# Column sums of x from the transposed blocks, and where the fold of W_self stands: a two-layer graph network on one core

## The chip, the core and the metric

The kernel runs on one core of a Trainium2 chip. The time is device microseconds of that core for one execution: the median of 3 runs of the kernel before is 706.46 us (703.6 to 707.98). The core has these engines, each with its own queue, worked off in order: TensorE (PE in the profile; its weight loads are PEld), VectorE (DVE), ScalarE (ACT), GpSimd (POOL) and SyncE (SP, which here only issues DMAs). GpSimd and ScalarE issue DMAs too.

## The reference

4096 nodes, 512 features, and an adjacency matrix in which about one entry in 1024 is set (some four neighbours a node). Layer 0 is graph attention with 8 heads of 64; layer 1 takes the mean over neighbours. Each ends with a residual sum and a layer norm without weights.

```python
# layer 0
Wh = einsum('nf,hfo->hno', x, W)
f1, f2 = Wh . a[:, :64], Wh . a[:, 64:]
e = where(adj > 0, leaky_relu(f1[:, :, None] + f2[:, None, :], 0.2), -9e15)
out = einsum('hnm,hmo->hno', softmax(e), Wh)
x = layernorm(x + out)
# layer 1
agg = mask @ x / max(deg, 1)
combined = concat([x @ W_self + b_self, agg @ W_nb + b_nb])
x = layernorm(x + relu(combined @ W_comb + b_comb))
```

Two things of it matter here. A node without a neighbour gets, by the softmax over equal values, the mean of Wh over all nodes, and this needs the column sums of x. And layer 1 is linear up to the relu, so W_self times the upper half of W_comb (called W_c1 here) and W_nb times its lower half can be multiplied once, ahead of time; the kernel calls this a fold, and the two products m1 and m2.

## The kernel before

The nodes are worked on in 32 blocks of 128 rows (NB = 32, P = 128). x stays in SBUF as `xs`. The order of all instructions is written out by hand: each engine works off its own in the order in which the Python code emits them. There are three stages.

**Stage 1 (lines 839 to 986), the lists.** Loop b over 29 blocks, the last ones behind it. For each block of 128 adjacency rows, SyncE loads two tiles of 1 MB (`load_adj`, four buffers `at`, issued two blocks ahead), ScalarE turns them into bf16 masks (`mask_adj`, L412), PE folds the masks into keys in PSUM (`fold_adj`, L430) which ScalarE first fills with column numbers (`key_bank`, L422), and VectorE picks the largest keys (`max_keys`, L445). Four blocks together are then decoded into lists of neighbours (`decode`, a generator that is taken a step at a time through `some(lists)`, four steps in a block); it is mostly small VectorE instructions (L454 to L538), and it ends by narrowing four tiles of owners to one byte (`of`, L516 on GpSimd for the first six groups, L518 on ScalarE for the others). `late_lists` adds a few steps from b = 16 on.

In the same loop a node block w is computed: `transposed` puts x transposed into PSUM (`tp`, one buffer, L346) and copies it to SBUF on ScalarE (`xT`, L348); `node_half` multiplies it with w_sb, twice (L354), VectorE copies each half out (L358), `node_rest` takes small pieces (L361, L362 on VectorE, L365 on GpSimd), and `store` writes the row to the table t0 in DRAM through GpSimd's DMA queue (L928). In two blocks, those in AHEAD = (14, 19), two node blocks are computed, so that the nodes end two blocks ahead of the lists. `sum_x` (L340) adds each block of x into `xacc` on GpSimd, four blocks after its load was issued. `mean_row` (from b = 25) makes the row for nodes without neighbours from it.

The fold of W_self lies here as well. `load_fold(0, ...)` loads W_self and W_c1, 1 MB each, ahead of the second block of x (L851). `fold_halves` is a generator that is taken one step in most odd blocks: `turned` transposes a quarter of W_self (L270) and copies it on ScalarE (L271) into parts of `xs` that are not loaded yet, PE multiplies in halves (L283), ScalarE copies the first half (L288) and VectorE adds the second (L290). `fold_bias` adds b_self times W_c1 into `brow`, four VectorE instructions (L322).

**Stage 2 (to line 1064), layer 0.** At its turn W_nb and the lower half of W_comb are folded in the same way in quarters (`fold_quarters`, L270, L303, L307). Then for each block five gathers of rows of t0 (`gather`, L610, each a DMA issued by GpSimd; five buffers), the attention weights, the sums on VectorE and PE (L692 to L720), a layer norm on ScalarE (L727 to L736), a transpose (L346), the product with m2 (`a_z`, L741), and two stores through SyncE: the product's row to t1, the transposed block to xt. `sum_bias` (i = 7) spreads `brow` over the partitions.

**Stage 3 (to line 1141), layer 1.** The same five gathers a block, now from t1. The first five blocks' gathers are limited to early rows, so that they can be issued before stage 2 has ended; six late gathers add the rest. Seven buffers: the gathers of block b + 7 follow `g_shared(b)` and `g_adds(b)`. PE does `g_self` (x times m1, eight matmul records of L773 a block) two blocks ahead and `g_shared` (L780, four records); VectorE and ScalarE do the rest (L754 to L800, `g_norm`).

The code of the functions follows; names there: `ps` is the PSUM pool, in which a tile of a name with `bufs=1` has to be read before the next of that name is written.

Of the kernel before, what the change touches and what calls it, by code (L numbers as in the profile page):

```python
# [31 lines left out]
F32 = mybir.dt.float32  # L32
# [8 lines left out]
P = 128  # L41
# [49 lines left out]
def listed_layers(  # L91
# [32 lines left out]
    EX = KX + 2 + 1  # L124
    AHEAD = (14, 19)
    FIRST = (0, 1, 3)
    LB = NB - 2

# [120 lines left out]

    def load_fold(k, w, fp, eng):  # L250
        wr = fp.tile([P, FB, HD], F32, name="wr")
        eng.dma_start(wr, w.rearrange("(c p) o -> p c o", p=P))
        wc = fp.tile([P, FB, HD], F32, name="wc")
        eng.dma_start(
            wc, w_comb[k * HD : (k + 1) * HD, :].rearrange("(c p) o -> p c o", p=P)
        )
        return wr, wc
# [9 lines left out]
    def turned(wr, c, wT):  # L267
        tp = ps.tile([P, FB, P], F32, name="sm", bufs=2)
        for d in range(FB):
            nc.tensor.transpose(tp[:, d, :], wr[:, c, ts(d, P)], ident)  # L270
        nc.scalar.copy(wT, tp.rearrange("p c r -> p (c r)"))  # L271
        return wT.rearrange("p (c r) -> p c r", c=FB)

    def fold_halves(loaded, m, place):

        wr, wc = loaded
        wT = turned(wr, 0, place(0))
        yield
        for c in range(FB):
            for k in range(2):  # L280
                mp = ps.tile([P, HD], F32, name="nm", bufs=2)
                for d in range(2 * k, 2 * k + 2):
                    nc.tensor.matmul(  # L283
                        mp, lhsT=wT[:, d, :], rhs=wc[:, d, :], start=(d == 2 * k),
                        stop=(d == 2 * k + 1),
                    )
                if k == 0:
                    nc.scalar.copy(m[:, c, :], mp)  # L288
                else:
                    nc.vector.tensor_add(m[:, c, :], m[:, c, :], mp)  # L290
                    if c + 1 < FB:
                        wT = turned(wr, c + 1, place(c + 1))
                yield

    def fold_quarters(loaded, m, place):

        wr, wc = loaded
        wT = turned(wr, 0, place(0))
        for c in range(FB):
            nxt = turned(wr, c + 1, place(c + 1)) if c + 1 < FB else None  # L300
            mp = ps.tile([P, HD], F32, name="tp", bufs=1)
            for d in range(FB):
                nc.tensor.matmul(  # L303
                    mp, lhsT=wT[:, d, :], rhs=wc[:, d, :], start=(d == 0), stop=(d == FB - 1)
                )
                if d == FB - 1:
                    nc.scalar.copy(m[:, c, :], mp)  # L307
                yield
            wT = nxt
# [27 lines left out]

    def sum_x(b, xacc):
        if b < NB:
            nc.gpsimd.tensor_tensor(xacc, xacc, xs[:, b, :], OP.add)  # L340

    def transposed(b, wp, tag="tp"):

        tp = ps.tile([P, FB, P], F32, name=tag, bufs=1)
        for c in range(FB):
            nc.tensor.transpose(tp[:, c, :], xs[:, b, ts(c, P)], ident)  # L346
        t = wp.tile([P, FB, P], F32, name="xT", bufs=2)
        nc.scalar.copy(t, tp)  # L348
        return t
# [18 lines left out]

    def mean_row(w_sb, xacc, wp):

        pm = ps.tile([P, FB], F32, name="sm", bufs=2)
        for c in range(FB):
            nc.tensor.matmul(
                pm[:, c : c + 1], lhsT=xacc[:, ts(c, P)], rhs=inv_n, start=True, stop=True
            )
        xm = small.tile([P, FB], F32, name="xm", bufs=1)
        nc.vector.tensor_copy(xm, pm)
        yield
# [68 lines left out]
    def decode(b0, dp, place):  # L447
# [66 lines left out]
        for g in range(G):  # L514
            if b0 + 2 * G < LB:
                nc.gpsimd.tensor_copy(of[:, b0 + g, :], sts[g])  # L516
            else:
                nc.scalar.copy(of[:, b0 + g, :], sts[g])  # L518
        nc.vector.tensor_copy(es[:, bs], pe[:, :, :, 0:EX])
# [296 lines left out]

    wp = ctx.enter_context(tc.tile_pool(name="work", bufs=1))
    fp_cm = tc.tile_pool(name="fold", bufs=1, side="right")
    fp = fp_cm.__enter__()
    oo_cm = tc.tile_pool(name="owners", bufs=1, side="right")  # L820
    oo = oo_cm.__enter__()
# [28 lines left out]
    brw = load_bias()  # L850
    loaded = load_fold(0, w_self, fp, nc.sync)  # L851
    load_x(1)
# [7 lines left out]
    nc.scalar.dma_start(brow[0:1, :], b_comb.rearrange("(a o) -> a o", a=1))  # L860
    xacc = xa.tile([P, FIN], F32, name="xacc")
    nc.gpsimd.memset(xacc, 0.0)
    pa = []
# [3 lines left out]
    nc.scalar.copy(av[:, 0], pa[0])  # L867
    xT = transposed(0, wp)

# [22 lines left out]
    summed(1, 1, pr1[1])  # L892
    m1s = fold_halves(loaded, m1, lambda c: xs[:, (NB - 12, NB - 11, NB - 4, NB - 3)[c], :])
    next(m1s)
    key_bank(0)
    for h in range(NH):
        mask_adj(0, h)
    bcol = bias_columns(brw)
    biased = fold_bias(loaded, bcol[:, 0:FB])
    for b in range(XL // 2):  # L900
        sum_x(b, xacc)

# [15 lines left out]
    def on_last(b):  # L918
        if b % G == 0:
            last[0] = fp.tile([P, FB, HD], F32, name="wc").rearrange(  # L920
                "p c (k r) -> p (c k) r", k=2
            )
        return last[0][:, b % G, :]
# [7 lines left out]
    for b in range(LB - 1):  # L931
        for k in range(1 + (b in AHEAD)):
            load_x(w + k + XL)
            sum_x(w + k + XL // 2, xacc)
        load_adj(b + 2, ap)
# [4 lines left out]
        for k in range(1 + (b in AHEAD)):  # L940
            nxt = transposed(w + 1, wp)
            if k == 0:
                key_bank(b + 1)
                for h in range(NH):
                    mask_adj(b + 1, h)
            node_block(w, xT, None if k else b)
            w, xT = w + 1, nxt
        for k in range(2):
            some(lists)
        if b == 0 or b % 2:  # L950
            next(m1s, None)
        if 1 <= b <= 4:
            next(biased)
        if b == 16:
            lates = late_lists(dp, fp.tile([P, FB * HD // P, P], F32, name="wr"))
        if b >= 16:
            next(lates, None)
        if b == 25:
            pieces = mean_row(w_sb, xacc, wp)
        if b >= 25:  # L960
            next(pieces, None)
# [5 lines left out]
    mask_adj(LB, 0)  # L967
    loaded = load_fold(1, w_nb, fp, nc.sync)
    fold_adj(LB - 1, dp)
# [13 lines left out]
    for k in range(4):  # L983
# [8 lines left out]
    gps += [gather_buffer(k) for k in range(2, GA)]  # L992
    m2 = loaded[0]
    m2s = fold_quarters(
        loaded, m2, lambda c: wp.tile([P, FW], F32, name="row", bufs=2)[:, 0:FIN]
    )
    a_owners(0, wp)
# [15 lines left out]
    for i in range(-2, NB + 1):  # L1013
# [45 lines left out]
        if i in (-1, 0):  # L1059
            for k in range(2):  # L1060
                next(biased)
        if i == 7:
            sum_bias()

# [16 lines left out]
    for b in range(2):  # L1081
# [3 lines left out]
        g_adds(b, G1[b], wq)  # L1085
        G1[b + GB] = gather(t1, b + GB, gps[b])
    for b in range(2):
        nxt = load_xT(b + 1, wp)
# [25 lines left out]
    for b in range(NB):  # L1114
# [20 lines left out]
        if b == 4:  # L1135
# [4 lines left out]
            nc.vector.tensor_add(flag, fl[:, 0:1], fl[:, 1:2])  # L1140
    g_norm(NB - 1, wp)
@with_exitstack
def dense_layers(
# [390 lines left out]
```

## Time and profile before

| | us |
|---|---|
| median of 3 runs | 706.46 |
| the profiled execution | 702.09 |
| its span, first to last instruction | 699.8 |
| mean granted clock of TensorE | 0.962 |
| PE busy, share of the span | 624.7 (89%) |
| DVE busy | 521.4 (75%) |
| ACT busy | 440.5 (63%) |
| POOL busy | 397.8 (57%), of which gathers L610 277.5 + 28.5, sum_x L340 40.9 |
| DMA | 209.64 MB, mean 300 GB/s |

The profile is of one execution. Its lines give for a group of instructions: the line of the kernel, engine, operation, output and inputs by the program's names, the shapes, the count, then busy time and the mean duration of one in ns, then the idle time of the engine just before them and what ended most of it. In the timeline a line is: start in us, duration, the same names, and in brackets the idle time before it and what ended it. In a table of stretches the columns are: start:end, length, busy us and count of PE, PEld, DVE, ACT and POOL, granted clock of TensorE (1.00 is full), the DMA engines' busy share, and GB/s. The busy time of PE is modelled, as its matmuls overlap. "issue" is time in which an engine waited for nothing that the profile shows.

The 40 slices of the page (17.5 us each) show where the stages lie:

```profile
GB/s 269 408 407 408 409 407 408 406 362 276 258 363 337 333 225 211 223 236 215 258 263 277 285 275 277 283 275 215 276 281 301 296 311 309 310 312 314 311 280 108
```

The first eight slices are stage 1 with the DMA at one constant rate, the next six the rest of stage 1 at lower rates; stage 2 begins in slice 15 or so, stage 3 in slice 29.

### The profile page before, as it was taken

To read this page: it belongs to the slowest core of one execution; us is meant where nothing else is said; L and a number is where in the kernel's file an instruction comes from. 1 tells how busy PE (TensorE), PEld (TensorE's weight loads), DVE (VectorE), ACT (ScalarE), POOL (GpSimd) and SP (SyncE) were. 2 spreads that over 40 slices of the span, in tenths; PEclk is the share of its full clock that TensorE was granted. 3 is DMA by queue.
4 is the path that set the end of the run, shared out by engine and by line. 5 is a ranking of instruction groups with operands and counts; after the bars stand their busy time and mean duration, and the time that the engine had idled before them with its cause. 6 is when DMAs were issued, how large, how long until landed. Compare 5 with 4: busy or idle time off the path is not lost. (4 is left out here: it accounts for less than half of the span.)

```text
span 699.8 us, 9126 instructions
## 1 busy us (share of the span) xinstructions
PE 624.7 (89%) x2350; PEld 345.6 (49%) x2350; DVE 521.4 (75%) x1416; ACT 440.5 (63%) x922; POOL 397.8 (57%) x468
## 2 busy tenths in 40 slices
PE   4899998977889787888999999999989999999982
PEld 2566666755567453454555555555434444444330
DVE  6258999896998885889889989989555566666552
ACT  1668878663767722566767777667536667676653
POOL 6342434323232277756667776756677777777771
PEclk9899999999999969899999999999999999999996
DMA  8999999997799977777888889986889899989983
GB/s 269 408 407 408 409 407 408 406 362 276 258 363 337 333 225 211 223 236 215 258 263 277 285 275 277 283 275 215 276 281 301 296 311 309 310 312 314 311 280 108
DMA packets 91973, 209.64 MB, mean 300 GB/s; under 512 B 13694, under 2 KB 13702, under 8 KB 91914
## 3 DMA queue, kind: packets, MB, share of 16 engines
q1 hardware_dynamic: 63024, 114.05, 44.2%
q0 software_dynamic: 28704, 94.66, 43.2%
q8 instruction: 21, 0.34, 0.2%
q14 instruction: 38, 0.31, 0.1%
q10 hardware_dynamic: 186, 0.28, 0.1%
HBM read 175.25 MB, written 33.69 MB: 299 GB/s over the span
## 5 line engine op out<-in xcount | busy, mean ns | idle before, releaser
L610 POOL DMA_INDIRECT g<-t,idx x290 | 277.5, 957 | 114.2 <-issue 54.6
L354 PE MATMUL pw<-w_sb,xT 128*128 128x264 f32 x512 | 135.5, 411 | 16.9 <-DVE row L358 16.9
L412 ACT ACTIVATE ab<-at 128x2048 bf16<-128x2048 int32 x64 | 122.0, 1908 | 29.6 <-DMA at<-in_adj_dram 20.8
L354 PEld LDWEIGHTS pw<-w_sb,xT 128*128 128x128 f32 x512 | 97.3, 200 | 47.5 <-DVE row L358 20.0
L741 PE MATMUL pw<-wr,xT 128*128 128x512 f32 x256 | 117.8, 603 | 0.7 <-ACT xT L348 0.7
L365 POOL COPY f1s<-lst 128x24 f32<-128x24 f32 x32 | 8.4, 262 | 136.9 <-DVE lst L361 69.1
L692 DVE TENSOR_TENSOR g<-g,key 128x1024 f32<-128x1024 f32 x64 | 77.9, 1217 | 1.1
L741 PEld LDWEIGHTS pw<-wr,xT 128*128 128x128 f32 x256 | 46.4, 191 | 47.3 <-issue 46.4
L704 PE MATMUL nm<-g,own 128*128 128x512 f32 x128 | 65.8, 638 | 0.0
L348 ACT COPY xT<-tp 128x512 f32<-128x512 f32 x64 | 37.4, 585 | 34.8 <-PE tp L346 34.7
L773 PE MATMUL nm<-m,xT 128*128 128x512 f32 x128 | 57.6, 593 | 1.5 <-DMA xT<-xt 1.5
L773 PE MATMUL pw<-m,xT 128*128 128x512 f32 x128 | 57.6, 593 | 0.0
L727 ACT ACTIVATE xs<-y,ln_sum 128x512 f32<-128x512 f32 x32 | 23.1, 722 | 48.6 <-DVE y L720 48.6
L346 PE MATMUL tp<-ident,xs 128*128 128x128 f32 x256 | 41.3, 286 | 10.5 <-ACT xs L736 8.1
L346 PEld LDWEIGHTS tp<-ident,xs 128*128 128x128 f32 x256 | 31.1, 147 | 36.5 <-ACT xs L736 24.6
L340 POOL TENSOR_TENSOR xacc<-xacc,xs 128x512 f32<-128x512 f32 x32 | 40.9, 1279 | 11.1 <-DMA xs<-in_x_dram 10.5
L358 DVE COPY row<-pw 128x264 f32<-128x264 f32 x64 | 27.1, 424 | 26.5 <-PE pw L354 21.3
L796 DVE SCALAR_TENSOR_TENSOR sm<-y,lst,nm 128x512 f32<-128x512 f32 x16 | 12.1, 756 | 38.7 <-PE nm L780 26.0
L773 PEld LDWEIGHTS nm<-m,xT 128*128 128x128 f32 x128 | 24.2, 190 | 32.4 <-issue 30.1
L773 PEld LDWEIGHTS pw<-m,xT 128*128 128x128 f32 x128 | 24.2, 190 | 30.8 <-issue 30.8
L610 POOL DMA_INDIRECT g<-t,idxe x30 | 28.5, 950 | 17.1 <-issue 6.4
L780 PE MATMUL pw<-g,own 128*128 128x512 f32 x64 | 31.5, 612 | 4.1 <-DMA g<-t,idx 3.1
(212 smaller groups left out, 1095.3 us busy)
## 6 DMA issues: line engine op xcount, KB each, us to landing
at<-in_adj_dram SPq DMA_DIRECT2D x64, 1024.0 KB, 10.7
t<-row POOLq DMA_DIRECT2D x32, 260.0 KB, 5.5
xt<-xT SPq DMA_DIRECT2D x32, 256.0 KB
t<-row SPq DMA_DIRECT2D x32, 256.0 KB, 3.7
xT<-xt SPq DMA_DIRECT2D x32, 256.0 KB, 5.3
out_dram<-row SPq DMA_DIRECT2D x32, 256.0 KB, 5.2
xs<-in_x_dram SPq DMA_DIRECT2D x31, 256.0 KB, 10.3
g<-t,idx POOLq DMA_INDIRECT x290, 4.7
```

The lines of the kernel that those rows point to most:

```text
L340: nc.gpsimd.tensor_tensor(xacc, xacc, xs[:, b, :], OP.add)
L346: nc.tensor.transpose(tp[:, c, :], xs[:, b, ts(c, P)], ident)
L348: nc.scalar.copy(t, tp)
L354: nc.tensor.matmul(pw, lhsT=xT[:, c, :], rhs=w_sb[:, c, k * HW : (k + 1) * HW], start=(c == 0), stop=(c == FB - 1),)
L358: nc.vector.tensor_copy(row[:, k * HW : (k + 1) * HW], pw)
L412: nc.scalar.activation(ab, loads.pop((b, h)), AF.Relu, accum_out=asum[:, b, h : h + 1])
L610: nc.gpsimd.indirect_dma_start(out=out, out_offset=None, in_=table, in_offset=bass.IndirectOffsetOnAxis(ap=at, axis=0),)
L692: nc.vector.tensor_tensor(gv if to is None else to.rearrange("p (k h d) -> p k h d", k=1, h=H), gv, E[b][:, sl].unsqueeze(3).to_broadcast( ...
L704: nc.tensor.matmul(NM[b], lhsT=OWN[b][:, k, :], rhs=G0[b][:, K0 + k, H:TW], start=False, stop=(k == KH - 1), skip_group_check=True,)
L741: nc.tensor.matmul(pz, lhsT=xT[:, c, :], rhs=m2[:, c, :], start=(c == 0), stop=(c == FB - 1))
L773: nc.tensor.matmul(NM[b], lhsT=xT[:, c, :], rhs=m1[:, c, :], start=False, stop=(c == FB - 1), skip_group_check=True,)
L780: nc.tensor.matmul(NM[b], lhsT=OWN[b][:, k, :], rhs=g[:, K0 + k, 0:HD], start=False, stop=(k == KH - 1), skip_group_check=True,)
```

## The change

1. `sum_x` and `xacc` go. `transposed` gets a place for sums: for even blocks VectorE sums the transposed block in PSUM along the nodes (one `tensor_reduce` of 128 x 4 x 128 to 128 x 4), for odd ones ScalarE copies it in four instructions of 128 columns that also accumulate. The last three blocks (29 to 31) are transposed once more in b = 23, 24 and 25, for their sums alone, and copied without sums later. `mean_row` then adds the 32 sums of each feature on VectorE, one block later than before.
2. The narrowing copies of the owners are all on ScalarE.
3. The fold of W_self leaves stage 1: its loads are issued at i = 7 of stage 2 (behind block 7's store, in SyncE's queue), its four bias steps come at i = 16 to 19 and `sum_bias` at i = 20, and its transposes and matmuls stand in the turn to stage 3, between the first two blocks' `g_shared` and the first `g_self`. `fold_halves` and `fold_quarters` become one function, `fold_weights`, which writes the product over the weights that it was made from. `turned` uses the PSUM tile `key` (one buffer) instead of `sm` (two).
4. AHEAD is (6, 13) instead of (14, 19).

```diff
-    AHEAD = (14, 19)
+    AHEAD = (6, 13)
+    EARLY = NB - 3
...
     def turned(wr, c, wT):
-        tp = ps.tile([P, FB, P], F32, name="sm", bufs=2)
+        tp = ps.tile([P, FB, P], F32, name="key", bufs=1)
...
-                    nc.scalar.copy(m[:, c, :], mp)
+                    nc.scalar.copy(wr[:, c, :], mp)
...
-    def sum_x(b, xacc):
-        if b < NB:
-            nc.gpsimd.tensor_tensor(xacc, xacc, xs[:, b, :], OP.add)
-
-    def transposed(b, wp, tag="tp"):
-
-        tp = ps.tile([P, FB, P], F32, name=tag, bufs=1)
+    def transposed(b, wp, sums=None, only=False):
+
+        tp = ps.tile([P, FB, P], F32, name="tp", bufs=1)
         for c in range(FB):
             nc.tensor.transpose(tp[:, c, :], xs[:, b, ts(c, P)], ident)
-        t = wp.tile([P, FB, P], F32, name="xT", bufs=2)
-        nc.scalar.copy(t, tp)
+        if only:
+            t = tp
+        else:
+            t = wp.tile([P, FB, P], F32, name="xT", bufs=2)
+        if sums is None or b >= EARLY and not only:
+            nc.scalar.copy(t, tp)
+        elif b % 2 == 0:
+            if not only:
+                nc.scalar.copy(t, tp)
+            nc.vector.tensor_reduce(sums[:, :, b : b + 1], tp, AX.X, OP.add)
+        else:
+            for c in range(FB):
+                nc.scalar.activation(
+                    t[:, c, :], tp[:, c, :], AF.Copy, accum_out=sums[:, c, b : b + 1]
+                )
         return t
...
-    def mean_row(w_sb, xacc, wp):
-
-        pm = ps.tile([P, FB], F32, name="sm", bufs=2)
-        for c in range(FB):
-            nc.tensor.matmul(
-                pm[:, c : c + 1], lhsT=xacc[:, ts(c, P)], rhs=inv_n, start=True, stop=True
-            )
+    def mean_row(w_sb, sums, wp):
+
         xm = small.tile([P, FB], F32, name="xm", bufs=1)
-        nc.vector.tensor_copy(xm, pm)
+        nc.vector.tensor_reduce(xm, sums, AX.X, OP.add)
+        nc.vector.tensor_scalar(xm, xm, 1.0 / N, None, OP.mult)
         yield
...
         for g in range(G):
-            if b0 + 2 * G < LB:
-                nc.gpsimd.tensor_copy(of[:, b0 + g, :], sts[g])
-            else:
-                nc.scalar.copy(of[:, b0 + g, :], sts[g])
+            nc.scalar.copy(of[:, b0 + g, :], sts[g])
...
-    loaded = load_fold(0, w_self, fp, nc.sync)
     load_x(1)
...
-            sum_x(w + k + XL // 2, xacc)
...
-            nxt = transposed(w + 1, wp)
+            nxt = transposed(w + 1, wp, sums)
...
-        if b == 0 or b % 2:
-            next(m1s, None)
-        if 1 <= b <= 4:
-            next(biased)
...
-        if b == 25:
-            pieces = mean_row(w_sb, xacc, wp)
-        if b >= 25:
+        if b in (23, 24, 25):
+            transposed(EARLY + b - 23, wp, sums, True)
+        if b == 26:
+            pieces = mean_row(w_sb, sums, wp)
+        if b >= 26:
             next(pieces, None)
...
         if i == 7:
+            loaded = load_fold(0, w_self, m1, weight(fc, "wc"))
+        if 16 <= i < 20:
+            if i == 16:
+                biased = fold_bias(loaded, bcol[:, 0:FB])
+            next(biased)
+        if i == 20:
             sum_bias()
...
         G1[b + GB] = gather(t1, b + GB, gps[b])
+    for _ in fold_weights(loaded, place):
+        pass
     for b in range(2):
         nxt = load_xT(b + 1, wp)
         g_self(b, xT, m1)
```

## The prediction

> **What bounds the kernel now.** I read the stages first, in one answer of busy times over five stretches (columns: PE, PEld, DVE, ACT, POOL busy with instruction counts, granted clock, DMA share, GB/s).
>
> ```profile
> 20.00:140.00 120.00, 110.58 (x596) 76.28 (x595) 92.43 (x294) 90.33 (x114) 44.87 (x66) 0.97 1.05 408
> 140.00:240.00 100.00, 84.52 (x466) 60.68 (x467) 86.58 (x310) 62.81 (x76) 29.70 (x54) 0.95 0.88 318
> ...
> 275.00:500.00 225.00, 214.11 (x764) 112.38 (x765) 200.94 (x463) 151.43 (x410) 150.92 (x158) 0.98 0.83 257
> 500.00:690.00 190.00, 179.57 (x415) 76.72 (x413) 106.84 (x237) 116.09 (x289) 138.95 (x147) 1.00 0.89 298
> ```
>
> Stage 1 (the lists, to 245 us) splits at 140. Before it the DMA runs full at 408 GB/s and sets the pace. After it the rate is 318: 100 us x 318 GB/s = 31.8 MB, which at 408 takes 77.9 us, so 22.1 us are lost to something else. VectorE is the busiest engine there after PE, whose busy time is modelled; ScalarE has 37 us free. Stage 2 (275 to 500) keeps PE full, stage 3 the GpSimd queue and PE.
>
> Why VectorE is so busy shows in the groups of stage 1 by shape (busy, mean ns) and in two pieces of the timeline (start, us):
>
> ```profile
> L503 DVE TENSOR_SCALAR lt<-iota,end 128x256 f32<-128x256 f32 x24 | 16.4, 682 | 0.8
> ...
> L531 DVE TENSOR_TENSOR jk<-jk,es 128x104 f32<-128x104 f32 x6 | 9.9, 1655 | 0.2
> ...
> L478 DVE TENSOR_SCALAR va<-nb 128x64 f32<-128x64 f32 x7 | 6.9, 980 | 0.2
> ```
>
> ```profile
> 103.99 1.42 POOL L516 CAST of<-own 128x256 uint8<-128x256 f32 x4
> ...
> 104.07 2.71 DVE L531 TENSOR_TENSOR jk<-jk,es 128x104 f32<-128x104 f32 x1
> ...
> 105.39 1.26 POOL L340 TENSOR_TENSOR xacc<-xacc,xs 128x512 f32<-128x512 f32 x1
> ```
>
> ```profile
> 175.40 0.27 DVE L531 TENSOR_TENSOR jk<-jk,es 128x104 f32<-128x104 f32 x1
> ```
>
> The same L531 takes 0.27 us alone and 2.71 while GpSimd casts and then adds: it ends when they end (106.7). Going through the timeline from 15 to 250 us, 26 VectorE instructions are over 1.4 times the median of their shape, and all 26 lie over an L340 or L516 of GpSimd. Their excess is 29.6 us, 11.9 of it after 140. The second loss is the block with two node blocks (b = 19): its masks are 17.6 us apart (156.82 to 174.41), and from 160 to 180 VectorE is busy 14.22 of 20 us at 228 GB/s.
>
> Then the end. In stage 3 GpSimd issues a gather every 1.25 us, 17 in 20 us, without a break from the early gathers on, and the chain that ended last goes back into that queue. PE starts layer 1 at 513.16, works without a hole at 5.15 us a block, and only near the end waits for gathers (PE's timeline; in brackets the wait):
>
> ```profile
> 513.17 3.70 PE L773 MATMUL nm<-m,xT 128*128 128x512 f32 x8 [1.47 <-DMA xT<-xt]
> ```
>
> ```profile
> 682.14 1.95 PE L780 MATMUL nm<-g,own 128*128 128x512 f32 x4 [1.14 <-DMA g<-t,idx]
> 687.16 2.79 PE L780 MATMUL pw<-g,own 128*128 128x512 f32 x4 [3.06 <-DMA g<-t,idx]
> ```
>
> **The change, part by part.** The sum is made against the profiled execution: 702.09 us, of which the span is 699.8. The median of the three timed runs, 706.46, is 0.6% above it.
>
> *Loads of W_self and W_c1 leave the start.* Two of 1 MB: 2.1 MB at 408 GB/s = 5.1 us, in a stretch where the DMA is the limit. **-5.1.** They return on SP's queue behind block 7's xt store in stage 2. The t1 and xt stores of the next blocks queue behind them; their tiles have two buffers, 13.7 us at 6.85 a block, and gathers are issued three blocks early. Taken as 0; without that cover up to the 5.1 itself, and I keep 2 for the range.
>
> *The fold leaves stage 1.* PE loses 2.9 (L270) + 15.9 (L283), ScalarE 8 copies of 0.57, VectorE 4 adds of 0.67 and 4 bias steps of 0.84. All lies before 125 us beside the full DMA: 0.
>
> *sum_x and the casts leave GpSimd.* 40.9 us (L340) and 9.7 (L516) off an idle engine: 0 by themselves. What counts is the excess on VectorE. Before 140 it is hidden by the DMA. After 140 VectorE has 86.6 - 11.9 (excess) - 1.2 (the node block of b = 19, now done earlier: two L358 of 0.42, L361, L362) + what is added. Added there: the reduce of tp. With both double blocks done early, blocks 18 to 28 transpose w = 21 to 31; four of the even ones are summed in the loop, one more in advance. No such reduce is in the trace; the nearest are L878, 1.21 us for 1024 columns, half of it 0.61, and L692 into PSUM, 0.69 for 512. I take 0.65, bounds 0.6 to 0.8: 5 x 0.65 = 3.3, and 0.3 for the new mean row. Sum 77.0. VectorE's idle time there was 13.4, of which 5.8 in the double block; 7.6 stay. 84.6 instead of 100: **-15.4.** DMA's floor for the same bytes, 77.9, and ScalarE lie below this, so VectorE with its handshakes stays late next.
>
> *ScalarE's added work.* An odd block trades one 512-column copy (L348, 0.585) for four of 128 columns with an accumulator. Copies of 8 columns take 0.145 (L316), of 256 about 0.40 (L637): 0.27 for 128. The accumulator's read is its own 0.188 us (L412), but it overlaps: masks that take 1.91 follow each other after 1.90. Bounds: 4 x 0.27 - 0.585 = +0.5 and 4 x (0.27 + 0.14 + 0.19) - 0.585 = +1.8; I take 4 x 0.41 - 0.585 = +1.05, nearer to the overlap seen. After 140: four odd blocks 4.2, two sums in advance 3.3, three groups of casts at 4 x 0.41 (L518) 4.9: 12.4, so 62.8 becomes 75.2 of 84.6. Before 140: 16 us on 90.3 of 120. Both fit: 0, and if they do not, this is the first rival.
> The Trainium skill ("Perfetto Trace Analysis", Optimizing Scalar/DVE Operations) speaks against this part: larger operations are better, since each pays an access overhead, about 51 ns for ScalarE on PSUM. By that page alone splitting in four costs 0.15 us a block, and the sum would not move, as ScalarE is hidden either way; no run here shows that overhead alone.
>
> *Sums of blocks 29 to 31 in advance* (b = 23 to 25). tp has one buffer, so PE's next transposes wait for ScalarE or VectorE, which come to it only after the block's masks or lists, and the next xT copy, queued before the next masks, waits for PE. Per block 0.60 of transposes and about 0.25 of handover on both sides = 1.1: **+3.3** (0 to 5; nothing, if the DMA is late there).
>
> *Double blocks at 6 and 13 instead of 14 and 19.* At b = 14 (122 to 128 us) the slices still show 407 GB/s, so a double block costs nothing while four adjacency tiles lie ahead: 0; up to 3.5 for both, as PE needs 10 us there against 6.45.
>
> *The turn to layer 0.* `turned` now has one PSUM buffer: the second turn waits for the first copy, 0.59 + 0.3: **+0.9.**
>
> *Stage 2.* Four bias steps of 0.84 in blocks 16 to 19, where VectorE is busy 18.1 of 20 us, 6.2 of 6.85 a block: 0.2 too much each, **+0.8** (0 to 3). sum_bias only moves from block 7 to 20.
>
> *The fold in the turn to layer 1.* The rows of the other fold give its pace:
>
> ```profile
> 259.92 0.60 PE L270 MATMUL sm<-ident,wr 128*128 128x128 f32 x4
> ...
> 260.76 3.70 PE L303 MATMUL tp<-wc,row 128*128 128x512 f32 x8 [0.24 <-ACT wr L307]
> ...
> 264.30 0.60 PE L270 MATMUL sm<-ident,wr 128*128 128x128 f32 x4
> ```
>
> 4.38 us for each quarter; first turns 0.6 + 0.9 + 0.4 and an uncovered copy before the last quarter 0.6: about 18.5. PE is free from 511.7, so g_self(0) starts at 530.2 instead of 513.2: 17.0 late. Its eight ScalarE copies lie in idle time. Two gatherings of buffers are ordered before the fold, but block 9's gathers need g_shared(2): 530.5 becomes 547.5, and GpSimd, which comes to them at 540.8, stands 6.7 us; afterwards PE (5.15 to 6.0 a block) is no slower than the gathers (6.2). PE itself has, from 650.99, seven g_shared of 1.72 and five g_self of 3.43 = 29.2 us left; 668.0 + 29.2 = 697.2 against 690.0 now. Both give **+7.2** (5 to 10).
>
> Sum: -5.1 - 15.4 + 3.3 + 0.9 + 0.8 + 7.2 = -8.3. Profiled 693.8; on the median 706.46 - 8.3 = **698.**
>
> A clock rule bears on this too. In the rows the granted clock is 0.95 from 140 to 240 and 1.00 in stage 3. The Trainium skill ("TensorE: Matmul & The Clock Gate", What's actually happening) says an idle window of some 3.4 us halves PE's clock; the trace agrees in kind, with 0.80 from 240 to 275, where PE waits most. A PE with the fold taken out of stage 1 could meet it oftener; an estimate from that page is 1.7 us for each such window, which no row here prices for the changed order.
>
> **Rivals.**
> 1. *Slower: ScalarE becomes the bound of stage 1.* The masks of 32 blocks run from 18.64 to 245.3, 7.08 us a block. ScalarE has 4.85 a block (0.48 + 0.52 + 1.90 + 1.95); at the upper bounds 0.9 and 0.41 more, 6.2, and it keeps its wait for tp (32.4 us over 32 L348, 1.0): 7.2. Then stage 1 gives -5.1 + 32 x 0.12 + 3.3 = +2.0; with 8.9 later +10.9: **717.** It decides above 7.0 a block, where the blocks no longer give the 3.8 that the loads leave open. For: the strict order of ScalarE's queue, and the sums ahead of the masks. Against: 37 us free after 140.
> 2. *No change: PE is next.* It is busy 84.5 of 100 after 140 and gets 1.8 of transposes for 4.5 of the node block moved away: 94 instead of 84.6 gives -5.1 - 6 + 3.3 + 8.9 = +1.1: **707.6.** For: 98% in 80 to 100. Against: busy PE is modelled.
> 3. *More: the DMA is the only bound of stage 1.* -5.1 - 22.1 + 0.9 + 5.2: -21: **685.** For: all engines near 77. Against: they wait for each other in turn.
> 4. *GpSimd is not the cause*: VectorE keeps its long instructions, 97 instead of 84.6: **710.** Against: 26 of 26.
>
> **How the numbers follow.** Forecast 0.45, rivals 0.17, 0.21, 0.13, 0.04. About 1% (7 us) is what a measurement of this kernel can tell from no change; 699.4 and 713.5 are the marks. The forecast with its bounds lies below the lower mark three times in four (0.35) and else between; with rival 3, faster has 0.48. Within 1%: 0.10 + 0.21 + 0.03 = 0.34, less 0.03 for rival 2's upper tail, 0.31. Slower: 0.17 + 0.04 = 0.21. The range 688 to 713 leaves out half of rival 3 and most of rival 1.
>
> **What would show it.** L531 and L503 at their short durations everywhere; the rate after 140 near 375 GB/s; the last mask some 17 us earlier; the span between stage 3's first and last g_self longer at its front by 17, a stand of about 7 us in the gathers before block 9, and no waits of PE for gathers at the end. It is wrong if ScalarE has no idle time from 140 on, if the double blocks drop the DMA rate at 6 or 13, or if the gathers never stand.

## The result, and the profile after

| | before | after |
|---|---|---|
| median, us | 705.17 (11 runs, 703.31 to 707.98) | 700.97 (11 runs, 699.45 to 703.0) |
| ratio, 95% interval | | 0.994 [0.9923, 0.9958] |
| the profiled execution | 702.09 | 699.45 |
| its span | 699.8 | 697.7 |

The change makes the kernel faster by 0.6%, 4.2 us, which lies within the 1% that the prediction took as no change; the two profiled executions differ by 2.6, as the one of before, 702.09, lies below all 11 timed runs. The forecast was 698 us, 8.3 us of gain. The answer of busy times by stretches, columns as before:

```profile
20.00:140.00 120.00, 106.38 (x594) 77.51 (x591) 84.77 (x337) 95.96 (x185) 14.29 (x38) 0.96 1.05 408
140.00:240.00 100.00, 80.30 (x450) 56.15 (x449) 77.41 (x311) 75.31 (x140) 14.69 (x32) 0.89 0.92 338
180.00:200.00 20.00, 13.65 (x64) 9.45 (x64) 12.73 (x48) 13.60 (x37) 1.54 (x4) 0.83 0.77 276
...
275.00:500.00 225.00, 217.84 (x763) 111.52 (x762) 194.20 (x447) 150.94 (x403) 150.97 (x157) 0.99 0.85 268
500.00:690.00 190.00, 184.55 (x441) 81.67 (x439) 105.95 (x236) 115.17 (x287) 131.94 (x139) 1.00 0.85 281
```

VectorE's busy time from 140 to 240 fell to 77.4 and ScalarE's rose to 75.3, as costed (though the stretch now holds 9 us behind the last mask, which ends at 230.94). But the rate there is 338 GB/s, not 375: no engine is full, and in 180 to 200 all of them drop together. That is a sign of waits, not of work. The page's 40 slices, 17.4 us each, show the DMA at its full rate up to 174 us now, 140 before, and the loss behind that:

```profile
GB/s 240 407 408 408 408 409 407 408 408 409 349 279 337 213 213 224 231 199 260 365 302 287 275 258 270 267 240 248 300 213 264 278 294 304 320 309 296 326 307 76
```

So the double blocks at 6 and 13 do not lower the rate. The long VectorE instructions, those stretched by GpSimd's work, are gone. The groups of stage 1 by shape, after:

```profile
L330 DVE TENSOR_REDUCE sums<-tp 128x4 f32<-128x512 f32 x15 | 10.2, 682 | 8.8 <-ACT xT L329 8.8
L486 DVE TENSOR_SCALAR lt<-iota,end 128x256 f32<-128x256 f32 x28 | 9.9, 355 | 1.0
L511 DVE TENSOR_TENSOR jk<-jk,es 128x104 f32<-128x104 f32 x7 | 1.9, 267 | 0.2
L461 DVE TENSOR_SCALAR va<-nb 128x64 f32<-128x64 f32 x7 | 1.4, 196 | 0.2
```

L486 is before's L503 (355 ns against 682), L511 is L531 (267 against 1655), L461 is L478 (196 against 980). Where the waits are shows PE's timeline from 176 to 202:

```profile
178.48 0.64 PE L320 MATMUL tp<-ident,xs 128*128 128x128 f32 x4
182.10 1.12 PE L320 MATMUL tp<-ident,xs 128*128 128x128 f32 x4 [2.99 <-ACT tp L333]
183.01 3.73 PE L341 MATMUL pw<-w_sb,xT 128*128 128x264 f32 x8
...
189.76 0.60 PE L320 MATMUL tp<-ident,xs 128*128 128x128 f32 x4
193.12 0.66 PE L320 MATMUL tp<-ident,xs 128*128 128x128 f32 x4 [2.76 <-DVE sums L330]
...
197.92 0.60 PE L320 MATMUL tp<-ident,xs 128*128 128x128 f32 x4
200.24 0.66 PE L320 MATMUL tp<-ident,xs 128*128 128x128 f32 x4 [1.73 <-ACT tp L333]
```

Each pair is a block's transposes for its sum in advance and then the loop's next ones, which must wait until ScalarE or VectorE has read the first out of tp. In the turn to layer 0 VectorE stands (its timeline), because the row tile that the last node block needs is still held by the mean row's DMA:

```profile
228.04 0.77 DVE L345 COPY row<-pw 128x264 f32<-128x264 f32 x2 [5.86 <-DMA t<-row]
```

In the turn to layer 1 the fold stands as forecast, from 501.04 to 519.38. PE's timeline there and at the end:

```profile
507.09 3.70 PE L281 MATMUL tp<-wc,row 128*128 128x512 f32 x8 [0.24 <-ACT m L285]
...
519.38 3.60 PE L753 MATMUL nm<-m,xT 128*128 128x512 f32 x8
```

```profile
682.78 1.88 PE L760 MATMUL nm<-g,own 128*128 128x512 f32 x4
684.49 1.88 PE L760 MATMUL pw<-g,own 128*128 128x512 f32 x4
```

The last two `g_shared` no longer wait for gathers (1.14 and 3.06 us before). GpSimd stands before block 9's gathers (its timeline; 0.30 is usual between issues). By block 13 it has lost 4.5 us against the kernel before; 6.7 were forecast:

```profile
532.28 0.94 POOL L590 DMA_INDIRECT g<-t,idx  x1 [2.54 <-ACT sm L734]
```

Read off at the same events in both profiled executions, the difference adds up as follows (the split of stage 1 uses the run pe_sums below):

| step | forecast | measured | from |
|---|---|---|---|
| loads out of the start | -5.1 | -4.2 | first mask 18.64 to 14.41 |
| stage 1 but for the next row | -15.4 | -18.8 | first to last mask 226.7 to 216.5: -10.1, less the 8.7 of the next row |
| sums of blocks 29 to 31 in advance | +3.3 | +8.7 | last mask 230.94, in pe_sums 222.24 |
| turn to layer 0 | +0.9 | +3.3 | last mask to first gather 1.16 to 4.41 |
| first gather to block 0's moments | 0 | -0.8 | 32.87 to 32.10 |
| stage 2 | +0.8 | +1.4 | moments of block 0 to the last a_z, 227.5 to 228.9 |
| fold, stage 3 to PE's end | +7.2 | +6.9 | 183.1 to 190.0 |
| behind PE's end | 0 | +1.5 | 9.9 to 11.4 |
| sum | -8.3 | -2.0 | spans 699.8 and 697.7, -2.1 |

Masks are counted from the start of the first to the end of the last; block 0's moments are the VectorE instruction ahead of its layer norm. The last masks of two kernels of the same time can lie 1.3 us apart (232.29 in casts_gp below), so the rows of stage 1 are no finer than that.

### The profile page after: what moved, and what is told of

The parts are those of the page before. It is cut to its first block, busy times and chain, and to the rows that moved or that the text cites. A ratio compares the mean times of both kernels' runs of the same rounds, so it can differ in the third digit from the quotient of the medians.

```text
span 697.7 us, 9203 instructions
## 1 busy us (share of the span) xinstructions
PE 627.3 (90%) x2354; PEld 346.8 (50%) x2354; DVE 498.3 (71%) x1429; ACT 457.8 (66%) x1060; POOL 346.9 (50%) x411
## 4 chain that ended last, share of the span: by engine, by line
PE 58%; DMA 17%; DVE 13%; ACT 5%; issue 4%; POOL 2%; SPq 1%; DVEq 0%; POOLq 0%; ACTq 0%
PE pw L721 13%; DMA at<-in_adj_dram 11%; PE pw L753 8%; PE nm L753 8%; PE nm L684 8%; PE nm L760 4%; PE pw L760 4%; PE pw L341 4%; PE tp L320 3%; DMA t<-row 2%; ACT ab L395 2%; PE tp L281 2%; DMA g<-t,idx 2%; PE sm L657 2%; DVE kk L428 2%
## 5 line engine op out<-in xcount | busy, mean ns | idle before, releaser
L341 PE MATMUL pw<-w_sb,xT 128*128 128x264 f32 x512 | 136.9, 415 | 7.4 <-issue 3.8
L684 PE MATMUL nm<-g,own 128*128 128x512 f32 x128 | 66.1, 641 | 0.0
L320 PE MATMUL tp<-ident,xs 128*128 128x128 f32 x268 | 44.2, 290 | 22.3 <-DVE sums L330 9.3
L320 PEld LDWEIGHTS tp<-ident,xs 128*128 128x128 f32 x268 | 32.6, 148 | 49.0 <-ACT xs L716 25.9
L776 DVE SCALAR_TENSOR_TENSOR sm<-y,lst,nm 128x512 f32<-128x512 f32 x16 | 12.1, 755 | 52.9 <-PE nm L770 29.2
L281 PE MATMUL tp<-wc,row 128*128 128x512 f32 x64 | 31.2, 630 | 1.6 <-ACT m L285 1.1
L760 PE MATMUL nm<-g,own 128*128 128x512 f32 x64 | 30.2, 594 | 1.2 <-ACT nm L744 1.2
L684 PEld LDWEIGHTS nm<-g,own 128*128 128x128 f32 x128 | 22.7, 198 | 16.3 <-issue 15.6
```

Source lines behind the costliest of these rows:

```text
L281: nc.tensor.matmul(mp, lhsT=wT[:, d, :], rhs=wc[:, d, :], start=(d == 0), stop=(d == FB - 1))
L341: nc.tensor.matmul(pw, lhsT=xT[:, c, :], rhs=w_sb[:, c, k * HW : (k + 1) * HW], start=(c == 0), stop=(c == FB - 1),)
L684: nc.tensor.matmul(NM[b], lhsT=OWN[b][:, k, :], rhs=G0[b][:, K0 + k, H:TW], start=False, stop=(k == KH - 1), skip_group_check=True,)
L760: nc.tensor.matmul(NM[b], lhsT=OWN[b][:, k, :], rhs=g[:, K0 + k, 0:HD], start=False, stop=(k == KH - 1), skip_group_check=True,)
```

## The experiments

Theory: both halves of the change work as forecast, but the sums in advance cost far more than their own work because of tp, and the turn to layer 0 has a wait of its own. Rivals: the fold's move pays for itself; ScalarE or PE is the bound of stage 1; GpSimd was not the cause. Medians of 5 to 12 runs each; all ratios are to the kernel before, whose median beside these runs lay between 703.92 and 705.25. A VectorE instruction is called long when it takes over 1.4 times the median of the same instruction in the changed kernel, and the rest of its time is its excess. By this the kernel before has 27, all over GpSimd's adds or casts, with 29.9 us of excess, 12.1 of it after 140.

**sums_only and fold_only: the two halves.** Edit of sums_only, on the changed kernel (`fold_halves` and its callers as before, and the loads and bias steps gone from stage 2):

```diff
+    loaded = load_fold(0, w_self, weight(fp, "wr"), weight(fc, "wc"))
     load_x(1)
...
+        if b == 0 or b % 2:
+            next(m1s, None)
...
-    for _ in fold_weights(loaded, place):
-        pass
```

> The changed kernel with the fold of W_self back in stage 1, as before (its two loads at the start, its pieces and four bias steps beside the masks); the sums and the casts stay off GpSimd. Theory (the two halves of the change work against each other): the loads come back, +4.2 us at the first mask; the fold leaves the turn to layer 1, -6.9; the bias steps leave blocks 16 to 19 of layer 0, -2. Together about 4.7 us below the changed kernel: 696 us, ratio to the kernel before 0.988. Rival (PE is the next bound of stage 1): the fold's 18.8 us on PE come back into a stage that has no room for them, the last mask comes 8 us or more later than the changed kernel's 230.9, and the time is 701 or above.

Measured: 695.48 us, 0.9862 [0.9836, 0.9888]: the theory's 696. First mask 18.38; first to last mask 216.9 us against 216.5 without the fold, so PE's 18.8 us cost 0.4 there. From the last a_z to PE's end 184.2 us, not 190.0.

fold_only is the mirror image, on the kernel before: the same lines the other way round.

> The kernel before with only the fold of W_self moved to the turn to layer 1 (loads at block 7 of layer 0, bias steps at blocks 16 to 19); the sums and casts stay on GpSimd, the double blocks at 14 and 19. Theory: first mask 4.2 us earlier, the long VectorE instructions stay (some 26 over GpSimd's), the last mask no more than 4 to 5 us earlier than 245.3; turn to layer 0 +1, bias steps +2, fold +7: 5 to 6 us above the kernel before, 710 us, ratio 1.008. Rival (the fold burdened stage 1, and its move makes up for itself): 705 or below, with the last mask 10 us or more earlier.

Measured: 707.48 us, 1.0039 [1.0021, 1.0057]. Slower, by less than expected (2.2 us, not 5 to 6); first mask 13.70, last 241.61, 24 long VectorE instructions over GpSimd's work with 29.1 us of excess. The profiled execution, 709.85, shows g_self(0) 23.0 us behind the last a_z, as in the changed kernel (6.3 before). So the fold's move costs: 2.2 us on the kernel before, 5.5 on the changed one (700.97 - 695.48).

**pe_sums: the sums in advance.** On the changed kernel:

```diff
-            transposed(EARLY + b - 23, wp, sums, True)
+            summed_early(EARLY + b - 23, sums)
...
+    def summed_early(b, sums):
+        pe = ps.tile([P, FB], F32, name="sm", bufs=2)
+        for c in range(FB):
+            nc.tensor.matmul(
+                pe[:, c : c + 1], lhsT=xs[:, b, ts(c, P)], rhs=onec, start=True, stop=True
+            )
+        nc.vector.tensor_copy(sums[:, :, b], pe)
```

> The changed kernel with the sums of blocks 29 to 31 made by PE: four matmuls of each block against a column of ones into a tile of its own in PSUM and a copy of 128x4 on VectorE, so that nothing waits for tp. Theory (the way through tp costs some 8 us, not the 3.3 of the prediction): PE's waits of 2.99, 2.76 and 1.73 us at 182, 193 and 200 us go, blocks 24 to 26 take 6 to 7 us instead of 10, 10 and 7, the last mask comes at 225 to 227 instead of 230.9, and the time is 4 to 5 us below the changed kernel, 696.5 us. Rival (the prediction's size): 1 to 2 us below it, 699.5, since DMA or VectorE sets the pace in those blocks anyway.

Measured: 688.22 us, 0.9777 [0.9752, 0.9802]: 12.8 us below the changed kernel (11.2 by the profiled spans), more than either expected. PE's timeline shows the sums (0.95 to 1.03 us a block, eight matmul records) with the next transposes right behind them:

```profile
179.49 1.03 PE L341 MATMUL sm<-onec,xs 128*128 128x1 f32 x8
180.39 0.63 PE L320 MATMUL tp<-ident,xs 128*128 128x128 f32 x4
...
185.16 0.95 PE L341 MATMUL sm<-onec,xs 128*128 128x1 f32 x8
185.97 0.63 PE L320 MATMUL tp<-ident,xs 128*128 128x128 f32 x4
```

and the stretch in which all engines had dropped is full (compare 13.65, 12.73, 13.60 and 276 GB/s):

```profile
180.00:200.00 20.00, 20.00 (x129) 15.20 (x129) 17.93 (x79) 18.11 (x30) 3.03 (x8) 1.00 1.04 391
```

Blocks 24 to 26 take 7.9, 5.1 and 5.6 us instead of 10.0, 10.0 and 7.1. The last mask comes 8.7 us earlier, the first gather 9.7, the last a_z 11.3. The edit takes the work of ScalarE and VectorE on these sums away together with the waits for tp; a second buffer for tp, which would part the two, was not run.

**own_row and pe_row: the mean row's tile.** own_row is the changed kernel with

```diff
-        mr = wp.tile([P, FW], F32, name="row", bufs=2)
+        mr = xa.tile([1, HD], F32, name="mr", bufs=1)
```

> The changed kernel with a tile of its own for the mean row, so that the last node block's copy on VectorE does not wait for the mean row's DMA. Theory (the turn to layer 0 loses its 3 us there): the wait of 5.86 us at 228 us goes, the first gather follows the last mask by about 1.5 us instead of 4.4, and the time is 2 to 3 us below the changed kernel, 698.5 us. Rival (the last lists hang on the last masks, the copy does not matter): first gather 4 us or more behind the last mask, time as the changed kernel's within 0.5 us.

Measured: 697.34 us, 0.9889 [0.9867, 0.9911]; first gather 1.46 us behind the last mask and 2.0 earlier than in the changed kernel. The theory holds, with 3.6 us where 2 to 3 were expected. pe_row has this edit and that of pe_sums:

> The changed kernel with both of the last two edits: sums of blocks 29 to 31 on PE, and the mean row in a tile of its own. Theory (two separate waits): both gains add, 688.2 less 3.6 = 684.6 us; the first gather follows the last mask by some 2 us instead of 3.4. Rival (with the masks ended at 222 the mean row is late itself, and the turn hangs on its two DMAs or on the last lists): 688, first gather as before at 225.6.

Measured: 689.6 us, 0.9785 [0.976, 0.981], the same as pe_sums alone, against the theory's 684.6. The first gather follows the last mask by 1.3 us instead of 3.4 and comes 0.75 us earlier, but the masks end 1.3 us later than in pe_sums, and the last a_z comes 2.1 us later. The gain of own_row does not add; why not was not settled.

**ahead_only and ahead_old: the double blocks.** One line each, `AHEAD = (6, 13)` on the kernel before, `AHEAD = (14, 19)` on the changed one.

> The kernel before with one line changed: the double blocks at b = 6 and 13 instead of 14 and 19; sums and casts stay on GpSimd. Theory of the prediction (the excess on VectorE is what holds stage 1 after 140 us, the double block only 1.2 us of node work): the long VectorE instructions stay, 702 to 703 us, ratio 0.996. Rival (the double block at 19 itself costs 10 us, its masks 17.6 us apart against 7, because no adjacency tile lies ahead by then): last mask 8 to 10 us earlier, 696 us, ratio 0.987.

Measured: 702.89 us, 0.9966 [0.9946, 0.9985], as the prediction's theory has it. 25 long instructions over GpSimd's work stay, with 28.8 us of excess, and the last mask ends at 245.31, as before.

> The changed kernel with the double blocks back at 14 and 19. Theory of the prediction: up to 2 us above the changed kernel, 702 us, since VectorE is rid of the excess. Rival (the double block at 19 costs by itself): masks 20 and 21 again some 14 to 17 us apart, the last mask 7 us or more later than 230.9, 707 us or above.

Measured: 704.81 us, 1.0004 [0.9987, 1.0022], 3.8 us above the changed kernel, between the two. Masks 20 and 21 are 12.4 us apart (7.9 in the changed kernel, 17.6 before), the last mask only 1.2 us later. The move is worth 2 to 4 us by itself.

**gp_extra and casts_gp: GpSimd.** gp_extra puts `sum_x` and its calls back into the changed kernel, and nothing reads `xacc`.

> The changed kernel with GpSimd's 32 adds of x into an accumulator of its own put back at their old places, though nobody reads the accumulator: only GpSimd's work comes back. Theory (GpSimd's operations stretch VectorE's, and VectorE holds stage 1 after 140 us): long VectorE instructions return, some 15 to 20 with 10 us of excess after 140 or less, the last mask 5 to 10 us later than 230.9, the time 706 to 711 us. Rival (GpSimd was not the cause, the gain came from the double blocks and the loads): 701 us within 1.

Measured: 713.4 us, 1.0126 [1.0098, 1.0153]: 12.4 us above the changed kernel, over the theory's range; last mask 244.92, 14.0 later. Eighteen long instructions, all over the adds, 23.0 us of excess, 8.8 after 140. Group of stage 1 by shape, and three lines of the timeline of all engines:

```profile
L510 DVE TENSOR_TENSOR jk<-iota,kx 128x104 f32<-128x104 f32 x6 | 9.3, 1544 | 0.2
```

```profile
186.86 1.96 DVE L490 TENSOR_SCALAR lt<-iota,end 128x256 f32<-128x256 f32 x1
187.37 1.29 POOL L318 TENSOR_TENSOR xacc<-xacc,xs 128x512 f32<-128x512 f32 x1
...
189.38 0.35 DVE L490 TENSOR_SCALAR lt<-iota,end 128x256 f32<-128x256 f32 x1
```

The same instruction takes 1.96 us over GpSimd's add and 0.35 after it. It starts 0.5 us ahead of the recorded start of the add, while GpSimd issues the store of a row; at 220.22, over such a store alone, it takes 0.35. The loss is larger than the excess after 140. Two things show where it comes from. Of the 14.0 us, 5.7 are there by block 18's mask (141.8 against 136.1): part of the loss lies before 140, where the kernel before hides its excess behind a DMA at 408 GB/s, while the rate from 20 to 140 is 397 here. And VectorE now also empties tp: PE's transposes in stage 1 wait 13.2 us for its sums here, 8.0 in the changed kernel, and ScalarE's summing copies, which stand ahead of masks in its queue, wait for the transposes. The group of these copies by shape, in the changed kernel and here:

```profile
L333 ACT ACTIVATE xT<-tp 128x128 f32<-128x128 f32 x56 | 14.5, 272 | 7.2 <-PE tp L320 5.5 <-DVE top L437 1.7
```

```profile
L337 ACT ACTIVATE xT<-tp 128x128 f32<-128x128 f32 x56 | 14.6, 276 | 18.6 <-PE tp L324 18.6
```

A rival is GpSimd's own queue, in which the adds stand ahead of the stores of rows. VectorE's waits for these stores grow less, from 10.2 to 13.4 us; the two were not tried apart.

The Trainium skill ("SBUF — State Buffer", Who interferes with whom) says that a VectorE instruction with two inputs in SBUF, or in a mode that uses both ports, and a GpSimd instruction that reads SBUF shut each other out for the whole instruction, and that a tensor_reduce on trn2 never contends. The runs agree on both: L510 has two such inputs (1.80 us in five of six, 0.27 alone), and the three of L334's reduces that overlapped an add took 0.67 to 0.69, as those that did not.

casts_gp puts the casts back:

```diff
-            nc.scalar.copy(of[:, b0 + g, :], sts[g])
+            if b0 + 2 * G < LB:
+                nc.gpsimd.tensor_copy(of[:, b0 + g, :], sts[g])
+            else:
+                nc.scalar.copy(of[:, b0 + g, :], sts[g])
```

> The changed kernel with the owners' casts back on GpSimd for the groups before the last two. Theory: 4 casts of some 1.4 us a group lie over VectorE's list work, so L511 and L486 grow again in the groups where they meet, about 1.3 to 2.4 us of excess a group and 4 to 6 after 140, while ScalarE is rid of 4.9 us that it had hidden: 2 to 4 us above the changed kernel, 704 us. Rival (ScalarE's added work was not hidden): 1 to 3 us below it, 699.

Measured: 700.95 us, 0.9941 [0.9918, 0.9964]: no difference from the changed kernel, and both expectations fall. VectorE gets 5.8 us of excess back, 3.1 after 140, and ScalarE is 4.4 us less busy there (70.9). The casts' move neither gained nor lost. So excess on VectorE is not a price by itself: casts_gp pays nothing for its 3.1 (unless ScalarE's 4.4 less make up for it), gp_extra more than its 8.8.

**pe_row_fold1, xt_sums and act_sums: a better version, and what bounds it.** pe_row_fold1 joins the edits of pe_row and sums_only.

> The same with the fold of W_self back in stage 1. Theory (the fold in the turn to layer 1 costs more than its loads, and stage 1 has room for it on PE while DMA is full): first mask 4.2 us later, turn to layer 1 7 us shorter, blocks 16 to 19 without bias steps 2 us shorter: 4 to 5 us below the version without it, 680 us, ratio 0.965. Rival (stage 1 is now so tight that PE has no room): the last mask 8 us or more later, the time 685 or above.

Measured: 686.0 us, 0.9722 [0.9696, 0.9749], 3.6 us below pe_row, where 4 to 5 were expected (680, from a pe_row of 684.6): first mask 5.0 us later, last mask 5.8. The fold belongs in stage 1 in this version too. xt_sums and act_sums are edits of it, in `transposed`:

```diff
-            nc.vector.tensor_reduce(sums[:, :, b : b + 1], tp, AX.X, OP.add)
+            nc.vector.tensor_reduce(sums[:, :, b : b + 1], t, AX.X, OP.add)
```

```diff
-        elif b % 2 == 0:
+        elif False:
```

> The best version so far (sums of blocks 29 to 31 on PE, a row of its own, the fold in stage 1; 686.0 us) with VectorE's reduce of the even blocks reading the copy xT in SBUF and not tp in PSUM, so that PE's next transposes wait for ScalarE's copy alone. Theory (PE's waits for VectorE's sums, 4.6 us there and 8.0 in the changed kernel, hold stage 1): these waits go, 2 to 4 us less, 683 us. Rival (the DMA's 408 GB/s sets the pace in the blocks concerned, or the reduce takes longer from SBUF): 686 within 1.

> The same best version with the sums of all blocks on ScalarE (four accumulating copies of 128 columns in every block). Theory: VectorE is rid of 15 x 0.68 us and PE's waits for its sums go; ScalarE gets 15 x 0.45 = 6.8 us more, 2.7 of it after 140, where it has 24 us free: 683 us, as with the reduce from xT or a little better. Rival (ScalarE's strict order makes it the bound, the prediction's first rival): 688 or above.

Measured: xt_sums 684.84 us, 0.9714 [0.9686, 0.9742], and act_sums 682.55 us, 0.9682 [0.9655, 0.9708], which its theory had at 683. In xt_sums PE's 4.6 us of waits for VectorE's sums are gone, and the time is not told apart from 686.0, so neither of its expectations is decided. act_sums is the fastest kernel here, 3.4 us below pe_row_fold1, its last mask 2.8 us earlier; its runs (681.88 to 683.86) lie below all of pe_row_fold1's (683.99 to 686.28), though the intervals of the ratios overlap. Its stretches:

```profile
140.00:240.00 100.00, 87.95 (x496) 62.27 (x493) 84.76 (x351) 78.85 (x159) 20.48 (x38) 0.91 0.99 371
180.00:200.00 20.00, 20.00 (x125) 15.59 (x124) 16.50 (x73) 18.56 (x39) 2.30 (x6) 0.91 1.03 391
200.00:220.00 20.00, 20.00 (x117) 13.55 (x118) 15.23 (x56) 15.40 (x21) 3.37 (x8) 1.00 1.03 386
```

DMA now stays near its 408 GB/s up to 220 (391 and 386), with PE full by its modelled time; which of the two is the bound there was not tried.

## Why the prediction was right, and where it was wrong

The time lies within the stated range and 3 us above the forecast, and that is in part luck: the gain is 4.2 us where 8.3 were forecast, and in the profiles 2.0. Row by row stage 1 came out 3.4 us better, and the sums in advance, the turn to layer 0 and the end 5.4, 2.4 and 1.5 worse. The likeliest outcome, faster by over 1% (0.48), did not come; within 1% had 0.31. The last mask comes 14.4 us earlier, not 17, and the rate after 140 is 338 GB/s, not 375.

*Right: GpSimd's adds cost stage 1 what was forecast or more.* gp_extra gives the same adds back and loses 12.4 us; the fourth rival falls. The forecast's -15.4 was even short: -18.8. Put back alone, the adds cost the masks 14.0 us (gp_extra) and the old double blocks 1.2 (ahead_old). These parts are no exact account of the kernel before: 5.7 of the 14.0 lie ahead of block 18, where that kernel ran its DMA full, as the prediction says. The casts, which the prediction counted with the adds, were worth nothing (casts_gp). The count of 26 long instructions hangs on the yardstick: by the medians of the kernel before itself, in which some shapes are long more often than not, it is 17 with 23.2 us, by the changed kernel's 27 with 29.9.

*Right: ScalarE's added work is hidden.* An odd block's four copies with accumulator cost about 0.5 us more than one copy (four starts in 1.01 us, the next instruction of ScalarE behind them, against 0.48 to the next behind the single copy), the lower bound named, and three times the 0.15 that the prediction estimated from a page. act_sums gives ScalarE more of them and gets faster; the first rival falls as a bound of stage 1, but its mechanism, the strict order of ScalarE's queue, shows in two of PE's three waits for tp. casts_gp says the same of the casts: they were free on ScalarE, but also brought nothing.

*Right: the fold's price, +7.2 (measured 6.9), and the 17.0 us by which it holds up g_self(0)* (16.7 of PE's time between the last a_z and it). Of the two ways to that price PE's holds; the gathers lost 4.5, not 6.7. sums_only shows that the loads' -4 does not pay for it: the change would have gained 9.8 us without this half.

*Not shown: PE is not next (second rival).* Its 707.6 did not come. But sums_only, in which PE gets 18.8 us more and the masks take 0.4 us longer, has all of that work before 123 us and says only that PE has room there. After 140 PE is busy 80.3 of 100 us in the changed kernel, and with the sums in advance out of tp 20.00 of 20 by its modelled time (pe_sums, 180 to 200, at 391 GB/s). The rival's 94 us follow from no row: 84.5 - 4.5 + 1.8 is 81.8.

*Wrong: "Sums of blocks 29 to 31 in advance", +3.3 (0 to 5).* The mechanism was named (tp has one buffer, and ScalarE and VectorE come to it only after the block's masks or lists), but priced at the work alone, 0.60 of transposes and handovers of 0.25. The waiting for a busy engine was left out of the sum: 2.99, 2.76 and 1.73 us by PE. With the slow matmuls behind the first of them, the last mask is 8.7 us late, and by pe_sums 12.8 us of the median (11.2 of the span) hang on these sums.

*Wrong: "The turn to layer 0", +0.9.* The one-buffer turn costs 0.68, near the forecast. The larger part was not seen: `mean_row` runs one block later, and its row tile is one of the two that the node blocks take in turn. The last node block's copy waits 5.86 us, with the last keys and lists queued behind it on VectorE. own_row took 3.6 us off; on top of pe_sums the same edit took off nothing, so what this wait is worth in a better version stays open.

*Wrong in size: "Stage 2", +0.8 (0 to 3).* Blocks 16 to 25 take 62.6 us in the changed kernel and in fold_only, 60.6 before and 60.8 in sums_only: the four bias steps cost 2.0, over half of their 3.4.

*Not in the sum: +1.5 behind PE's end.* It belongs to the fold's move: from PE's end to the last instruction there are 11.4 us here and 11.5 in fold_only, 9.9 before and 10.1 in sums_only. With PE full to the end the last two blocks' work comes back to back; that this is the reason is argued, not tried.

The third rival (DMA as the only bound of stage 1, 685) comes nearest to what the changed kernel is without the sums in advance through tp (688.22 in pe_sums), and without the wait for the row tile as well (689.6 in pe_row).

## What to carry to other kernels

Before giving a step to another engine, look at which buffer it will hold, and count from when the reading engine is free, not from when the data are: here sums through a PSUM tile with one buffer, priced at 1.1 us a block, took about 2.9. A change can hold two halves of opposite sign; run each half alone before judging it. That GpSimd is idle does not make tensor work on it free: look for VectorE instructions of one shape with two durations.

## What the hardware showed that was not expected

PE's clock fell within one short wait. Behind the wait of 2.99 us at 182.10 the four transposes took 1.12 us instead of 0.66, and the eight matmuls 3.73 instead of 1.95; behind the wait of 2.76 at 193.12 they were at full speed. In pe_sums a wait of 2.17 us (164.4 to 166.57) was followed by slow ones as well, 1.12 for the four. The length of the wait alone does not tell the two apart. The granted clock, the last number but two of each line, does:

```profile
178.00:181.30 3.30, 1.11 (x10) 0.87 (x9) 3.13 (x14) 3.24 (x11) 0.74 (x2) 1.00 1.05 407
181.40:188.10 6.70, 6.00 (x21) 3.87 (x22) 2.69 (x10) 4.51 (x16) 0.00 (x0) 0.50 0.84 314
188.20:194.90 6.70, 3.94 (x22) 3.26 (x21) 5.19 (x22) 2.65 (x5) 0.80 (x2) 1.00 0.95 338
```

It is half from 181.32 to 188.15, 6.83 us. In all these traces the half-clock stretches start a whole number of steps of 3.41 us apart and last 3.41 us or a multiple of it (6.83, 13.65, 17.07), but for the last one of a run. So the steps lie on a grid of their own. Of the first wait 2.21 us fell into one step (177.91 to 181.32); the second was cut by the end of a step at 191.56 into 1.20 and 1.56; in pe_sums 2.09 us fell into one. Idle time of PE is still not all of it: in act_sums PE is busy by its modelled time throughout, and the clock falls all the same:

```profile
180.40:183.70 3.30, 3.30 (x31) 3.27 (x30) 2.64 (x14) 2.34 (x3) 0.75 (x2) 1.00 1.04 406
183.80:187.10 3.30, 3.30 (x12) 2.11 (x14) 3.04 (x10) 3.30 (x16) 0.00 (x0) 0.50 1.05 393
```

The step of the first line holds sixteen matmuls of 24 columns (1.86 us) and eight of one column (1.03), few columns for their time; whether such work counts as idle was not tried.

The Trainium skill ("TensorE: Matmul & The Clock Gate", What's actually happening) puts the idle window at some 3.4 us and calls it free-running; the grid of 3.41 us and the halving agree with that, but the steps ahead of the falls at 181.32 and in act_sums were not idle throughout (PE busy 1.11 and 3.30 of 3.30 us), so that PE has to be idle for the whole window is not borne out by its modelled busy time.

A copy with accumulator on ScalarE costs more in place. Two lines of ScalarE's timeline after, out of tp into xT, and two within tp:

```profile
183.26 0.28 ACT L333 ACTIVATE xT<-tp 128x128 f32<-128x128 f32 x1 [1.21 <-PE tp L320]
...
183.53 0.27 ACT L333 ACTIVATE xT<-tp 128x128 f32<-128x128 f32 x1
```

```profile
180.48 0.26 ACT L333 ACTIVATE tp<-tp 128x128 f32<-128x128 f32 x1
...
180.88 0.26 ACT L333 ACTIVATE tp<-tp 128x128 f32<-128x128 f32 x1
```

Each takes 0.26 to 0.28 us, but the next starts 0.27 us later in the first case and 0.40 in the second; whether that is the place or the same tile as input and output was not tried.
